# The attention layer of a four-layer graph network: products of two steps grouped, chain stages cut elsewhere, the last 1024 nodes split by block

## The chip, the cores and the metric

The kernel runs on one core of one Trainium2 chip. The metric is the device time of one execution in microseconds (us). The engines are named as in the profile: PE (TensorE; PEld is its weight load), DVE (VectorE), ACT (ScalarE), POOL (GpSimd) and SP (SyncE, which only issues DMAs here). Each engine works through its own queue in order. A name with a q, such as PEq, is an engine's sequencer.

## The reference

Four graph layers on 4096 nodes with 128 features; `adj` is a 4096 x 4096 float32 matrix. After each layer `x = layernorm(x + layer(x))`.

- Layer 0: a signed attention over the graph. Layer 1: two Chebyshev convolutions of order 3 with ELU.
- Layer 2, "the third layer" of this study, is a four-head attention (heads h of 32 features):

```
hp      = (x @ weight.T), seen as (n, 4, 32)
C[n,m]  = alpha_src[m] + alpha_dst[n]          (per head)
tau     = adj.T * exp(max(0.2 C, C))
z       = sum over n of adj.T * (tau / tau_sum) * hp,  + bias
```

- Layer 3: `h @ W_self + (adj @ h / deg) @ W_neigh`, with `deg` the row sums of `adj`.

## The kernel before, in words

Sources are cut into 32 tiles of 128 nodes (`nt`), targets into 8 blocks of 512 (`IB`) or 4 wide blocks of 1024 (`WB`). A matrix `adjT` is read in chunks of 1 MB (512 x 512), `adj` in 1 MB tiles of 2 x 128 sources by 1024 targets. Both land in one ring of five buffers (`ld`, tile `chunk`); SP issues these loads in order, each when its buffer is free.

Layers 0 and 1 run first, up to the product with `w` (L861), the last big product of layer 1. This product is the **block loop** (L855): for each of 8 blocks `ib`, 32 matmuls over 8 chunks into one PSUM bank `pp`. From there on the order of PE, DVE, ACT and POOL is written out by hand: inside `manual_schedule` (L795 to L904) each of these engines gets its instructions in the order in which the program emits them. Four kinds of work are interleaved.

1. **Chains**: generators in a queue, advanced by one stage with `one(chains)`. `block_end` (L588) finishes a block of layer 1: ELU (the helper at L498), transposes, statistics, normalization, `xT`, and with it the per-source factors `es`, `cs` and features `hc` of layer 2. `block_targets` (L629) makes the per-target factors `dv`. `targets` (L669) spreads them over partitions into `D`. `finish` (L712) divides numerators by denominators; `layer3_blocks` (L732) normalizes and multiplies with the weights of layer 3, giving `y`. All of them use one PSUM bank, `px`.
2. **Steps** (L682): one source tile for one pass. A pass (class `Heads`) is 2 heads for 1024 targets; there are 8 passes of 32 steps, 256 in all. A step has two `scalar_tensor_tensor` on DVE (L688, 128 x 1024, `max(D, es) * a`) that give `tau`, and `tau2 = tau * a`, of which DVE makes 704 columns (L691) and POOL 320 (L692) and 1024 (L693). `a` is a PSUM copy of the `adj` tile, made by ACT (L666), which sums the degrees beside it. `tau` and `tau2` have three buffers each. The first two passes go in turn and share a load and a copy for their first 24 source tiles.
3. **Products** (L696, L823): four matmuls of 32 columns each for the denominators (from `tau`) and four for the numerators (from `tau2`), side by side in PE's columns, summed over the pass in the PSUM banks `den` and `num`. After each step PE does the denominators of the step before it and the numerators of the one before that.
4. **Pieces**: single matmuls of the layer-3 product `adj @ y` (L759) for 1024 sources at a time. `credit` (L886) lets 1.3 of them in after each step. They begin when `layer3_blocks` of a wide block has run. What a product sums in PSUM goes into `acc3` (L773, L775). The last 1024 sources' product (L905) comes after the hand-ordered part and also makes the output (`layer3_out`, L780).

In the block loop, 1 step follows a chunk (2 the last) from block 3 on, for source tiles whose block has been finished. PSUM has eight banks: `den`, `num`, `pp`, `px`, two for `a`, two for the first pass's sums, which later become the second `a`.

Of the kernel before, what the change touches and what calls it, by code (L numbers as in the profile page):

```python
# [11 lines left out]
F32 = mybir.dt.float32  # L12
# [7 lines left out]
P = 128  # L20
# [13 lines left out]
def adj_resnorm_d4(ctx: ExitStack, tc: tile.TileContext, x_in, xT_in, adj, adjT, w0g, w0gT, a0, w1a, b1a,  # L34
# [56 lines left out]
    deg = const.tile([P, NT, NW], F32, name="deg")  # L91
# [383 lines left out]
    def network(usual):  # L475

        with ExitStack() as whole:
# [98 lines left out]

            ps_nd = enter(name="ps_nd", bufs=1, space=PSUM)
# [9 lines left out]

            def block_end(ib, p):  # L588
# [3 lines left out]
                oT = l1w.tile([P, IB], F32, name="t2T")  # L592
                nc.vector.tensor_add(oT, p, h0T[:, blk])
# [19 lines left out]
                yield  # L613
                yield
                for half in range(2):
                    two = slice(ib * TB + 2 * half, ib * TB + 2 * half + 2)
                    pn = ps_x.tile([P, 2, F + H], F32, name="px")
                    for k in range(2):
                        t = ib * TB + 2 * half + k
                        nc.tensor.matmul(pn[:, k, :], xT[:, t * P:(t + 1) * P], W2S, start=True, stop=True)  # L620
                    nc.scalar.activation(cs[:, two, :], pn[:, :, F:F + H], AF.Exp, scale=0.2)
                    nc.scalar.activation(es[:, two, :], pn[:, :, F:F + H], AF.Exp, scale=0.8)
                    for k in range(2):
                        t = ib * TB + 2 * half + k
                        nc.vector.tensor_mul(hc[:, t], pn[:, k, 0:F].rearrange("p (h f) -> p h f", f=FO),
                                             cs[:, t, :][:, :, None].to_broadcast([P, H, FO]))
                    yield

            def block_targets(ib):  # L629
# [9 lines left out]
                nc.vector.tensor_sub(d, d, dv[:, blk])  # L639
                nc.scalar.copy(dv[32:64, blk], d[32:64, :])  # L640
                nc.scalar.copy(dv[64:96, blk], d[64:96, :])
                yield
                nc.vector.tensor_sub(d[64:96, :], d[64:96, :], dv[64:96, blk])
                nc.scalar.copy(dv[64:96, blk], d[64:96, :])
                yield
# [4 lines left out]
            class Heads:  # L650
# [3 lines left out]
                def __init__(self, mp, hp):  # L654
                    self.mp, self.hp = mp, hp
                    self.D, self.made = None, 0
                    self.sums = ps_first if (mp, hp) == (0, 0) else ps_nd

                def load(self, nt):

                    if nt % 2 == 0:
                        self.a2 = ld.tile([P, 2, WB], F32, name="chunk")
                        nc.sync.dma_start(self.a2, adj[self.mp, nt // 2])
                    a = self.a2[:, nt % 2, :]
                    ap = ps_a[nt % len(ps_a)].tile([P, WB], F32, name="a")
                    nc.scalar.activation(ap, a, AF.Copy, accum_out=deg[:, nt, self.mp:self.mp + 1])  # L666
                    return a, ap

                def targets(self, mbs=range(2)):  # L669
                    if self.D is None:  # L670
                        self.D = l2w.tile([P, 2, 2, IB], F32, name="D", bufs=2)
                    for mb in mbs:
                        for h in range(2):
                            d = ps_x.tile([P, IB], F32, name="px")
                            nc.tensor.matmul(d, selD[:, 2 * self.hp + h, :],
                                             dv[:, self.mp * WB + mb * IB:self.mp * WB + (mb + 1) * IB],
                                             start=True, stop=True)
                            nc.scalar.copy(self.D[:, h, mb, :], d)
                            self.made += 1
                            yield  # L680

                def step(self, nt, a, ap):  # L682

                    assert self.made == 4
                    tau = l2w.tile([P, 2, WB], F32, name="tau", bufs=3)
                    tau2 = l2w.tile([P, 2, WB], F32, name="tau2", bufs=3)
                    for h in range(2):
                        nc.vector.scalar_tensor_tensor(tau[:, h, :], self.D[:, h].rearrange("p b i -> p (b i)"),  # L688
                                                       es[:, nt, 2 * self.hp + h:2 * self.hp + h + 1], ap,
                                                       op0=ALU.max, op1=ALU.mult)  # L690
                    nc.vector.tensor_tensor(tau2[:, 0, 0:OWN], tau[:, 0, 0:OWN], ap[:, 0:OWN], ALU.mult)  # L691
                    nc.gpsimd.tensor_tensor(tau2[:, 0, OWN:WB], tau[:, 0, OWN:WB], a[:, OWN:WB], ALU.mult)  # L692
                    nc.gpsimd.tensor_tensor(tau2[:, 1, :], tau[:, 1, :], a, ALU.mult)  # L693
                    return tau, tau2

                def product(self, is_den, nt, r):  # L696
# [5 lines left out]
                    for h in range(2):  # L702
                        for mb in range(2):
                            q = 32 * (2 * h + mb)
                            nc.tensor.matmul(acc[q:q + 32, :], weights(nt, 2 * self.hp + h, is_den),  # L705
                                             r[:, h, mb * IB:(mb + 1) * IB], start=nt == 0, stop=nt == NT - 1)
                    if nt == NT - 1:
                        if is_den:
                            self.nd = l2w.tile([P, 2, IB], F32, name="nd")
                        nc.scalar.copy(self.nd[:, int(is_den), :], acc)  # L710

                def finish(self):  # L712
# [5 lines left out]
                    yield  # L718
                    q = transpose4(ps_x, "px", lambda k: self.nd[:, 0, k * P:(k + 1) * P])
                    yield  # L720
                    z = l2w.tile([P, TB, 2, 2, FO], F32, name="z")
                    nc.vector.tensor_mul(z.rearrange("p k h b f -> p (k h b) f"),
                                         q.rearrange("p k (g f) -> p (k g) f", f=FO),
                                         rd.rearrange("p k g -> p (k g)")[:, :, None].to_broadcast([P, TB * 4, FO]))
                    for mb in range(2):
                        xb = x[:, (2 * self.mp + mb) * TB:(2 * self.mp + mb + 1) * TB,
                               2 * self.hp * FO:(2 * self.hp + 2) * FO].rearrange("p k (h f) -> p k h f", f=FO)
                        eng = nc.vector if (self.mp, self.hp) == (NW - 1, H // 2 - 1) else nc.gpsimd
                        eng.tensor_tensor(xb, z[:, :, :, mb, :], xb, ALU.add)
                    yield  # L730

            def layer3_blocks(mp):  # L732
# [3 lines left out]
                for j in range(2):  # L736
                    b = 2 * mp + j
                    q = transpose4(ps_x, "px", lambda k: x[:, b * TB + k, :])
                    xb = l2w.tile([P, TB, P], F32, name="xb", tag="z")
# [5 lines left out]
                    yield  # L745
                    nc.vector.reciprocal(sj, sj)
                    for half in range(2):
                        q = ps_x.tile([P, 2, 2, F], F32, name="px")
                        for k in range(2):
                            nc.tensor.matmul(q[:, k].rearrange("p s f -> p (s f)"), xb[:, 2 * half + k, :],  # L750
                                             W3.rearrange("p s f -> p (s f)"), start=True, stop=True)
                        for k in range(2):
# [4 lines left out]
                        yield  # L757

            def layer3_product(mp):  # L759


                for ib in range(NB):
                    blk = slice(ib * IB, (ib + 1) * IB)
                    last = mp == NW - 1
                    p = (ps_nd.tile([P, IB], F32, name="num") if last and ib % 2 else ps_p.tile([P, IB], F32, name="pp"))
                    for c in range(2):
                        a = chunk(ld, adjT, ib, 2 * mp + c)
                        for k in range(TB):
                            nc.tensor.matmul(p, y[:, (2 * mp + c) * TB + k, :], a[:, k, :],  # L769
                                             start=c == 0 and k == 0, stop=c == 1 and k == TB - 1)  # L770
                            yield c == 1 and k == TB - 1
                    if mp == 0:
# [20 lines left out]

            acc3 = state.tile([P, N], F32, name="acc3", tag="yn")
            with tc.manual_schedule(engines={mybir.EngineType.PE, mybir.EngineType.DVE, mybir.EngineType.Activation,  # L795
# [4 lines left out]
                passes = [Heads(mp, hp) for mp in range(NW) for hp in range(H // 2)]  # L800
                held = NT - 2 * TB
                todo = deque((heads, nt) for nt in range(held) for heads in passes[0:2])
                todo += [(heads, nt) for heads in passes[0:2] for nt in range(held, NT)]
                todo += [(heads, nt) for heads in passes[2:] for nt in range(NT)]
                steps = len(todo)
                ahead = passes[0].load(0)
                credit = 0.0
# [10 lines left out]
                def start_product(mp):  # L818
                    pieces.append(layer3_product(mp))
                    return  # L820
                    yield

                def products():  # L823

                    if len(behind) > 1:
                        heads, nt, tau, _ = behind[-2]
# [116 lines left out]
```

The softmax here doesn't subtract the row's maximum and nothing guards it: scores larger than these inputs give would overflow.

## Time and profile before

| what | before |
|---|---|
| median of 6 runs | 2281.26 us (2277.09 to 2282.76) |
| the profiled execution, whole | 2284.24 us |
| its span, first to last instruction | 2282.3 us |
| busy in the span: PE, PEld | 2175.7, 843.2 us |
| busy: DVE, ACT, POOL | 1176.7, 593.6, 836.9 us |
| mean granted PE clock | 0.99 |
| `w` product (block loop) | from 1113 to 1465 us |
| steps (L688 to L691) | from 1211 to 2189 us |
| end of the span | 2282 us |

A timeline line reads: start, duration, engine, source line, operation, output<-inputs, shapes, count, and in brackets how long the engine stood idle before it and what released it. A line of the chain of waits has start, duration and the engine and line that held the end back in that stretch. A window line has the stretch, its length and the busy time of each engine with the number of instructions. PE's busy time includes instructions that are queued in the array, so a full PE need not be at its peak. A float32 matmul appears as two records.

### The profile page before, as it was taken

The numbers are of one execution on the slowest core, as the hardware profiler recorded it, in microseconds if no ns is written. First come the engines' busy times: TensorE is split into PE (matmuls) and PEld (weight loads), VectorE is DVE, ScalarE is ACT, GpSimd is POOL, SyncE is SP. The second block draws the span as 40 slices with busy tenths as digits, with TensorE's granted clock in tenths as the row PEclk, the third lists the DMA queues.
The fourth block names the chain that finished last, engine by engine and source line by source line (L and its number), as shares of the span: only waits on it lengthen the run. The fifth ranks groups of instructions, "written<-read, shape, count | busy, mean of one in ns | idle before, by whom it ended". The sixth has DMA issues, their size and how long they took to land.

```text
span 2282.3 us, 22715 instructions
## 1 busy us (share of the span) xinstructions
PE 2175.7 (95%) x8552; PEld 843.2 (37%) x8552; DVE 1176.7 (52%) x1709; ACT 593.6 (26%) x1012; POOL 836.9 (37%) x540
## 2 busy tenths in 40 slices
PE   3899999999999999999999999969999999999998
PEld 2333444444444444444443333312222322232233
DVE  4544463000001100000025776779999999999955
ACT  4755200000000000000032222334444443443320
POOL 0000000000000000000004565669999999999930
PEclk9799999999999999999999999999999999999999
DMA  7886647888776677777776555434666666666665
GB/s 266 331 330 237 221 170 267 300 298 303 265 270 229 235 264 238 267 263 275 273 243 226 216 185 210 177 111 148 221 247 241 232 238 244 243 234 241 236 225 204
DMA packets 83608, 549.14 MB, mean 241 GB/s; under 512 B 9376, under 2 KB 15520, under 8 KB 17568
## 3 DMA queue, kind: packets, MB, share of 16 engines
q1 hardware_dynamic: 75200, 542.15, 67.4%
q10 hardware_dynamic: 8288, 5.44, 0.8%
q8 instruction: 69, 1.13, 0.2%
q14 instruction: 51, 0.42, 0.1%
HBM read 545.46 MB, written 2.10 MB: 240 GB/s over the span
## 4 chain that ended last, share of the span: by engine, by line
PE 83%; DVE 10%; issue 3%; ACT 2%; DMA 2%; ACTq 0%; POOL 0%; DVEq 0%; POOLq 0%
PE pacc L514 29%; PE pacc L346 10%; PE den L705 9%; PE pp L769 9%; PE pp L861 8%; PE num L705 7%; DVE tau L688 5%; DVE tau L691 2%; PE pmm L540 2%; PE num L769 1%; PE pden L334 1%; PE num L861 1%; PE px L135 1%; PE ptr L135 1%; ACT a L666 1%
## 5 line engine op out<-in xcount | busy, mean ns | idle before, releaser
L688 DVE SCALAR_TENSOR_TENSOR tau<-D,es,a 128x1024 f32<-128x1024 f32 x512 | 629.2, 1268 | 27.7 <-ACT a L666 27.5
L693 POOL TENSOR_TENSOR tau<-tau,chunk 128x1024 f32<-128x1024 f32 x256 | 609.1, 2379 | 16.6 <-DVE tau L688 15.8
L612 POOL TENSOR_TENSOR x<-x,B2R 128x512 f32<-128x512 f32 x8 | 10.2, 1280 | 1180.8 <-PE px L135 1180.8
L705 PE MATMUL den<-tau,cs 128*32 128x512 f32 x2048 | 357.4, 608 | 30.8 <-DVE tau L688 22.9
L666 ACT ACTIVATE a<-chunk 128x1024 f32<-128x1024 f32 x232 | 238.7, 1029 | 453.2 <-DVE tau L691 387.8
L705 PE MATMUL num<-tau,hc 128*32 128x512 f32 x2048 | 346.4, 599 | 0.6 <-POOL tau L693 0.6
L692 POOL TENSOR_TENSOR tau<-tau,chunk 128x320 f32<-128x320 f32 x256 | 222.5, 869 | 155.7 <-DVE tau L688 106.3
L769 PE MATMUL pp<-chunk,xT 128*128 128x512 f32 x448 | 236.1, 629 | 0.0
L691 DVE TENSOR_TENSOR tau<-tau,a 128x704 f32<-128x704 f32 x256 | 223.9, 875 | 0.0
L514 PE MATMUL pacc<-chunk,t 128*128 128x512 f32 x512 | 223.5, 592 | 0.0
L514 PE MATMUL pacc<-chunk,v 128*128 128x512 f32 x512 | 222.5, 592 | 0.0
L514 PE MATMUL pacc<-chunk,x 128*128 128x512 f32 x512 | 221.9, 593 | 0.0
L861 PE MATMUL pp<-chunk,w 128*128 128x512 f32 x448 | 208.1, 602 | 2.4 <-ACT xT L565 1.6
L346 PE MATMUL pacc<-chunk,hw 128*128 128x512 f32 x408 | 196.3, 621 | 2.3 <-DVE hw L411 2.3
L705 PEld LDWEIGHTS den<-tau,cs 128*32 128x32 f32 x2048 | 58.1, 107 | 270.0 <-DVE tau L688 179.7
L705 PEld LDWEIGHTS num<-tau,hc 128*32 128x32 f32 x2048 | 88.9, 110 | 145.0 <-issue 131.5
L514 PEld LDWEIGHTS pacc<-chunk,v 128*128 128x128 f32 x512 | 97.2, 190 | 122.0 <-issue 122.0
L514 PEld LDWEIGHTS pacc<-chunk,x 128*128 128x128 f32 x512 | 96.4, 190 | 116.7 <-issue 116.7
L514 PEld LDWEIGHTS pacc<-chunk,t 128*128 128x128 f32 x512 | 96.1, 190 | 115.3 <-issue 115.3
L769 PEld LDWEIGHTS pp<-chunk,xT 128*128 128x128 f32 x448 | 71.7, 188 | 158.6 <-issue 144.3
L561 DVE COPY w<-ptr 128x512 f32<-128x512 f32 x8 | 5.5, 691 | 241.5 <-PE ptr L135 241.5
L861 PEld LDWEIGHTS pp<-chunk,w 128*128 128x128 f32 x448 | 80.5, 190 | 115.5 <-issue 111.4
(190 smaller groups left out, 1442.7 us busy)
## 6 DMA issues: line engine op xcount, KB each, us to landing
chunk<-in_adjT SPq DMA_DIRECT2D x386, 1024.0 KB, 4.8
chunk<-in_adj SPq DMA_DIRECT2D x116, 1024.0 KB, 4.8
keep<-in_adjT SPq DMA_DIRECT2D x13, 1024.0 KB, 6.9
xT<-in_xT ACTq DMA_DIRECT2D x8, 256.0 KB, 6.3
out<-o ACTq DMA_DIRECT2D x8, 256.0 KB, 4.3
W1A<-in_w1a ACTq DMA_DIRECT2D x1, 384.0 KB, 5.9
W1B<-in_w1b ACTq DMA_DIRECT2D x1, 384.0 KB, 6.7
W0T<-in_w0gT ACTq DMA_DIRECT2D x1, 64.0 KB, 5.6
```

The lines of the kernel that those rows point to most:

```text
L135: nc.tensor.transpose(p[:, k, :], src(k), ident)
L346: nc.tensor.matmul(p, hw[:, j * TB + k, :], a[:, k, :], start=first and k == 0, stop=last and k == TB - 1)
L514: nc.tensor.matmul(p, stationary(c * TB + k), a[:, k, :], start=n == 0 and k == 0, stop=n == NB - 1 and k == TB - 1)
L540: nc.tensor.matmul(ph, W1A[:, k, hh * P:(hh + 1) * P], r, start=k == 0, stop=k == 2)
L666: nc.scalar.activation(ap, a, AF.Copy, accum_out=deg[:, nt, self.mp:self.mp + 1])
L688: nc.vector.scalar_tensor_tensor(tau[:, h, :], self.D[:, h].rearrange("p b i -> p (b i)"), es[:, nt, 2 * self.hp + h:2 * self.hp + h + 1], ap,
L691: nc.vector.tensor_tensor(tau2[:, 0, 0:OWN], tau[:, 0, 0:OWN], ap[:, 0:OWN], ALU.mult)
L692: nc.gpsimd.tensor_tensor(tau2[:, 0, OWN:WB], tau[:, 0, OWN:WB], a[:, OWN:WB], ALU.mult)
L693: nc.gpsimd.tensor_tensor(tau2[:, 1, :], tau[:, 1, :], a, ALU.mult)
L705: nc.tensor.matmul(acc[q:q + 32, :], weights(nt, 2 * self.hp + h, is_den), r[:, h, mb * IB:(mb + 1) * IB], start=nt == 0, stop=nt == NT - 1)
L769: nc.tensor.matmul(p, y[:, (2 * mp + c) * TB + k, :], a[:, k, :], start=c == 0 and k == 0, stop=c == 1 and k == TB - 1)
L861: nc.tensor.matmul(p, w[:, c * TB + k, :], a[:, k, :], start=c == 0 and k == 0, stop=c == NB - 1 and k == TB - 1)
```

## The change

Five edits, all in layer 2 and what follows it; line numbers above are those of the kernel before.

- **Products**: two steps are emitted, then one group: the numerators of the older pair's second step, denominators and numerators of the new pair's first step, denominators of its second step. Pieces follow by credit, 2.67 for a pair, and 4 for a pair in the last pass; after the end of a product's sum (`wait`) the accumulation goes in after the next step.
- **Chain stages** now end just after PE's instructions, and what the other engines do with them opens the next stage. `block_end`'s first stage (the ELU, now with `min`, `Exp`, `Relu` in that order) is emitted at once, ahead of the group. `block_targets` works in place in PSUM.
- **Block loop**: steps stand ahead of the chunk's matmuls and halfway through them. Blocks 4 to 7 have five cuts with two steps each (10 steps), block 3 four (8). A step's load and copy are emitted right before it.
- **First two passes** go in turn to the end and share all loads and copies.
- **Last 1024 nodes**: two passes of 4 heads for 512 targets each (`Pass` with `wide` false) replace two of 2 heads for 1024. A step there has four `scalar_tensor_tensor` of 512 columns; the `tau2` parts keep their sizes as 2 x 352, 2 x 160 and 2 x 512; two steps share one `a` tile; loads are two DMAs of half the columns. Block 6's layer-3 product then becomes pieces within block 7's pass, and only block 7's remains for the end.

```diff
             def block_end(ib, p):
                 oT = l1w.tile([P, IB], F32, name="t2T")
+                r = l1w.tile([P, IB], F32, name="elu_r")
+                n = l1w.tile([P, IB], F32, name="elu_n")
                 nc.vector.tensor_add(oT, p, h0T[:, blk])
-                elu(oT, oT, B1B)
+                nc.vector.tensor_scalar(n, oT, B1B, 0.0, op0=ALU.add, op1=ALU.min)
+                nc.scalar.activation(n, n, AF.Exp)
+                nc.scalar.activation(r, oT, AF.Relu, bias=B1B)
+                nc.vector.scalar_tensor_tensor(oT, n, -1.0, r, op0=ALU.add, op1=ALU.add)
                 yield
                 q = transpose4(ps_x, "px", lambda k: oT[:, k * P:(k + 1) * P])
+                yield
                 nc.vector.tensor_add(x[:, tb, :], q, x[:, tb, :])
...
+                q = transpose4(ps_x, "px", lambda k: x[:, ib * TB + k, :])
                 yield
-                q = transpose4(ps_x, "px", lambda k: x[:, ib * TB + k, :])
                 nc.scalar.copy(xT[:, blk], q.rearrange("p k i -> p (k i)"))
...
                         nc.tensor.matmul(pn[:, k, :], xT[:, t * P:(t + 1) * P], W2S, start=True, stop=True)
+                    yield
                     nc.scalar.activation(cs[:, two, :], pn[:, :, F:F + H], AF.Exp, scale=0.2)
...
             def block_targets(ib):
-                d = l1w.tile([96, IB], F32, name="elu_r")
-                nc.scalar.activation(d, pd, AF.Exp, scale=-0.8)
-                nc.scalar.copy(dv[:, blk], d)
                 yield
+                nc.scalar.activation(pd, pd, AF.Exp, scale=-0.8)
+                nc.scalar.copy(dv[:, blk], pd)
                 yield
-                nc.vector.tensor_sub(d, d, dv[:, blk])
+                nc.vector.tensor_sub(pd, pd, dv[:, blk])
...
+                    for q in range(0, 4, n):
+                        head = self.parts[q][0]
+                        nc.vector.scalar_tensor_tensor(flat(tau[:, q:q + n]), flat(self.D[:, q:q + n]),
+                                                       es[:, nt, head:head + 1], ap, op0=ALU.max, op1=ALU.mult)
...
+                        own = OWN // 2
+                        rep = lambda v, q: v[:, None, :].to_broadcast([P, q, v.shape[1]])
+                        nc.vector.tensor_tensor(tau2[:, 0:2, 0:own], tau[:, 0:2, 0:own], rep(ap[:, 0:own], 2), ALU.mult)
+                        nc.gpsimd.tensor_tensor(tau2[:, 0:2, own:IB], tau[:, 0:2, own:IB], rep(a[:, own:IB], 2), ALU.mult)
+                        nc.gpsimd.tensor_tensor(tau2[:, 2:4, :], tau[:, 2:4, :], rep(a, 2), ALU.mult)
...
-                passes = [Heads(mp, hp) for mp in range(NW) for hp in range(H // 2)]
-                held = NT - 2 * TB
+                passes = [Pass([2 * mp, 2 * mp + 1], [2 * hp, 2 * hp + 1]) for mp in range(NW - 1) for hp in range(H // 2)]
+                passes += [Pass([b], list(range(H))) for b in range(NB - 2, NB)]
...
+                def products():
+                    if len(behind) > 2:
+                        this, nt, _, tau2 = behind.popleft()
+                        num(this, nt, tau2)
+                    this, nt, tau, tau2 = behind.popleft()
+                    this.product(True, nt, tau)
+                    num(this, nt, tau2)
+                    this, nt, tau, _ = behind[0]
+                    this.product(True, nt, tau)
...
+                    cuts = [0, 2, 4, 6, 8] if ib < 4 else [0, 2, 4, 5, 6, 8]
+                    for first, last in zip(cuts, cuts[1:]):
+                        ks = [(c, k) for c in range(first, last) for k in range(TB)]
+                        for n, (c, k) in enumerate(ks):
+                            if ib > 2 and n in (0, len(ks) // 2):
+                                if n == 0:
+                                    load()
+                                step()
...
+                            if n + 1 in (len(ks) // 2, len(ks)) or ib <= 2 and k % 2:
                                 one(chains)
+                        if last == NB:
+                            end = block_end(ib, p)
+                            next(end)
+                            chains.append(end)
...
+                        if ib > 2:
+                            products()
+                load()
...
                 while todo:
                     step()
-                    credit = min(credit + 1.3, 2.0) if pieces else 0.0
-                    while credit >= 1.0:
+                    if wait:
+                        wait = bool(pieces) and not one(pieces)
...
+                    load()
                     one(chains)
+                    step()
+                    load()
+                    products()
+                    one(chains)
+                    credit = min(credit + (4.0 if todo and todo[0][0] is passes[-1] else 2.67), 4.0) if pieces else 0.0
+                    while credit >= 1.0 and pieces and not wait:
                         credit -= 1.0
-                        if one(pieces):
-                            credit = 0.0
-                    one(chains)
...
-            for _ in layer3_product(NW - 1):
+            for _ in layer3_product(this.blocks):
                 pass
```

More of the change, by code (lines that the diff above doesn't have):

```diff
@@ L682, in step @@
                 def step(self, nt, a, ap):
                     assert self.made == 4
[L685 to L690, printed above, removed]
@@ L840, in step @@
                 def step():
-                    nonlocal ahead
-                    heads, nt = todo.popleft()
-                    tau, tau2 = heads.step(nt, *ahead)
+                    this, nt = todo.popleft()
+                    assert nt // TB in ended
+                    tau, tau2 = this.step(nt, *ahead)
+                    behind.append((this, nt, tau, tau2))
                     if nt == NT - 1:
-                        later = passes.index(heads) + 2
+                        later = passes.index(this) + 2
@@ L846, in step, with num @@
                         if later < len(passes):
                             chains.append(passes[later].targets())
-                    if todo and not (todo[0][1] == nt and heads is passes[0]):
-                        ahead = todo[0][0].load(todo[0][1])
-                    behind.append((heads, nt, tau, tau2))
-                    products()
-                ready = 0
+                def num(this, nt, tau2):
+                    this.product(False, nt, tau2)
+                    if nt == NT - 1 and this is not passes[-1]:
+                        if this is passes[0]:
+                            first_sums.close()
+                            ps_a.append(enter(name="ps_a2", bufs=1, space=PSUM))
+                        chains.append(this.finish())
+                        if this.heads[-1] == H - 1:
+                            chains.append(layer3_blocks(this.blocks))
+                            chains.append(start_product(this.blocks))
@@ L899, in network @@
                 nc.vector.reciprocal(rdeg, rdeg)
-                for chain in (heads.finish(), layer3_blocks(NW - 1)):
+                for chain in (this.finish(), layer3_blocks(this.blocks)):
                     for _ in chain:
```

207 lines of the change are left out of this document (97 added, 110 removed).

## The prediction, made before the changed kernel had been run

> **What bounds the kernel now.** I read the busy windows of the attention part first, then the timeline of a few steps in it, then the chain of waits at its two ends. Before 1113 us (layers one and two up to `w`) nothing changes.
>
> The windows give stretch, length, busy time and count of PE, PEld, DVE, ACT, POOL, then granted clock, DMA share, GB/s:
>
> ```profile
> 1400.00:1450.00 50.00, 47.71 (x223) 16.54 (x221) 33.93 (x45) 14.34 (x27) 27.73 (x18) 1.00 0.56 196
> 1450.00:1500.00 50.00, 38.87 (x194) 11.97 (x190) 35.74 (x47) 13.81 (x26) 30.98 (x20) 0.93 0.35 126
> 1600.00:1700.00 100.00, 98.99 (x570) 28.98 (x568) 100.00 (x98) 42.43 (x79) 99.63 (x65) 1.00 0.63 228
> 1900.00:2000.00 100.00, 99.34 (x571) 28.30 (x570) 100.00 (x99) 38.96 (x68) 98.36 (x63) 1.00 0.68 247
> ```
>
> In the 1400s PE leads, around 1500 nobody does, and from 1600 PE, DVE and POOL all look full. The timeline tells these three apart:
>
> ```profile
> 1703.61 2.46 DVE L688 SCALAR_TENSOR_TENSOR tau<-D,es,a 128x1024 f32<-128x1024 f32 x2
> 1705.99 0.88 DVE L691 TENSOR_TENSOR tau<-tau,a 128x704 f32<-128x704 f32 x1
> 1706.79 2.46 DVE L688 SCALAR_TENSOR_TENSOR tau<-D,es,a 128x1024 f32<-128x1024 f32 x2
> ```
>
> DVE starts a step every 3.18 us without a gap (two instructions 1.19 apart, then 0.80); POOL's two take 3.16. On PE the chain of waits gives 1.00 for the four denominator matmuls, 0.86 for the four numerators and 1.06 for one piece of the layer-3 product, 2.91 together, and 0.86 more when there are two pieces. A full matmul is two records of 0.43, that is 0.86; four narrow ones side by side also take 0.86. The excess is changeover: 0.14 into the narrow ones, 0.20 back. At 1.3 pieces a step PE needs 3.17. So **DVE bounds** from 1538 (59th step) to 2189 (256th): 198 x 3.18 = 629 of 651 us, the other 22 being DVE's own chain work. PE has almost the same load but does not hold DVE up.
>
> Before that PE bounds, with a hole at every block's end:
>
> ```profile
> 1303.82 3.65 PE pp L861 x8
> 1307.49 0.70 DVE t2T L593
> 1308.21 0.72 ACT elu_r L501
> 1308.94 0.53 ACT elu_n L503
> 1309.49 0.69 DVE t2T L504
> 1310.18 2.40 DVE tau L688 x2
> ```
>
> The next step's DVE work is queued behind the block's ELU, which waits for PE's last matmul. PE has one held step to do and then starves: some 3.3 us a block. Blocks 4 to 7 take 209.0 us (1255.7 to 1464.7), 52.25 each, with 9 steps each. The drain after them is slow because each of the last 16 steps of the first two passes loads and copies its own `a` into one PSUM buffer:
>
> ```profile
> 1495.57 0.88 DVE L691 TENSOR_TENSOR tau<-tau,a 128x704 f32<-128x704 f32 x1
> 1496.49 1.03 ACT L666 ACTIVATE a<-chunk 128x1024 f32<-128x1024 f32 x1 [3.40 <-DVE tau L691]
> 1497.74 2.47 DVE L688 SCALAR_TENSOR_TENSOR tau<-D,es,a 128x1024 f32<-128x1024 f32 x2 [1.28 <-ACT a L666]
> ```
>
> 4.56 a step (1493.18 to 1497.74), 1.38 of it DVE waiting for the copy. From 2189.0, the last step's end, to 2282.3 is the tail: 93.3 us, bound by PE at 7.45 a block (16 records, 6.87, and transposes, 0.58).
>
> **The change, part by part.** The times are the profiled execution's (span 2282.3, 2284.24 whole); the median of the six runs is 2281.26, 3 less, and I take the difference over to it.
>
> *Block loop.* `load` leaves the place before the loop, where its ACT copy (1.15) stood ahead of `xT` on the chain: -1.2. Block 3 goes from 47.4 us to 27.5 + 8 x 1.72 + 4 x 0.34 + 2.6 = 45.2 on PE, taken 46: -1.4. Blocks 4 to 7 have 10 steps in 5 groups: PE 27.5 + 17.2 + 1.7 + 2.6 (transposes, `px`, `pd`) = 49.0, the floor. DVE: 10 x 3.18, 5 x 1.38 for the copy, 6.5 of chain work (add 0.60, ELU 1.1, x add 0.69, statistics 1.6, `hc` 1.0, rest 1.5) = 45.2, to which come waits for ACT: the ELU's 1.2, the square root's 0.4 and the normalization's 1.65, which now stands ahead of the next `a` copy in ACT's queue: 48.5. The ELU is now queued behind two steps, where POOL is at work. A row that shows what this can cost:
>
> ```profile
> 1509.40 2.37 POOL L693 TENSOR_TENSOR tau<-tau,chunk 128x1024 f32<-128x1024 f32 x1 [0.27 <-DVE tau L688]
> 1510.03 2.28 DVE L639 TENSOR_TENSOR elu_r<-elu_r,dv 96x512 f32<-96x512 f32 x1
> ```
>
> With POOL idle that line takes 0.69 (its minimum); here it ends half a microsecond after POOL's. Three of a block's instructions read SBUF this way (clamp, ELU sum, mean), so 0 to 1.6 each, which puts the ceiling at 53.3; L639 itself moves to PSUM and is in the 6.5 at 0.60. The second `px` matmul now follows `hc` of the first within one stage: nothing if DVE is ahead, else `es`, `cs` and `hc`, 0.9. So floor 49, ceiling 54. SP's queue gets each step's load ahead of its chunks; at a DMA share of 0.56 and 4.8 to land I cost that at nothing, five buffers covering it (a late one would show as ACT's copy waiting for a DMA, 4.8 at most). The Trainium skill speaks of the port in "SBUF — State Buffer", Who interferes with whom: the loser of the shared port waits for the whole other instruction. By that rule each could wait up to POOL's 2.4, an estimate of 56 a block. From the rows, and nearer to the floor since POOL is not always in its long instruction, I take 51: -5 (-13 to +7), and 48 steps are done at the loop's end near 1457, where before there were 44. The hole at the block's end goes, since `products` follows the ELU with 3.4 us of held matmuls; if DVE is late there, the hole returns.
>
> *Drain.* Before, from 1464.7 to the 64th step's end at 1555.8: 91.1 us for 20 steps. After, 16 steps in 8 pairs sharing `a`: 2 x 3.18 + 1.38 = 7.74, with 5 more for the last ELU, 67 in all: -24 (-18 if all chain work adds up, -28 if it fits the copy waits).
>
> *Products of two steps together, in the 128 wide steps.* PE per pair: 4 x 0.86 + 0.34 + 2.67 x 0.86 = 6.07 against DVE's 6.36. It was no bound before, so this is 0; what hides it is DVE's load. If DVE were 0.3 a pair faster, PE would be late next.
>
> *Last 1024 nodes as two passes of four heads.* 64 steps have four 512-element instructions in place of two of 1024. That form is not in the trace. Nearest: L785, same operation, 332 ns at 128, and 1265 at 1024: 1.04 ns an element and 199 fixed, of which about 75 overlap, so 0.66 each; the low end is L775's 0.60 for 512, the high end 0.73, nothing overlapping. 4 x 0.66 + 0.80 = 3.43, so +0.25 x 64 = **+16** (+1 to +35; the elements stay the same, so there is no gain, and I take the fit, which is drawn through the same operation). The skill's "VectorE: DVE Perf Modes", The TRN2 errata — SBUF-src ops pay a fixed extra latency per instruction, speaks against this part too: small tiles pay the fixed cost anew, about 150 cycles; by that, an estimate of +20. POOL's pieces keep their sizes (320 and 1024), and L612 with a repeated operand is on its line (1280 for 512), so POOL stays under 3.43. ACT's copies halve and 20 MB of loads go (with the drain's), both off the path. The narrow load is two DMAs in 2 KB runs, a form not in the trace; at twice the 4.8 us it would still land within the 13.7 of the four steps that it serves, so 0; if it were three times as long, some 0.2 a step. Counting the loop out, the product of blocks 4 and 5 gives 28 pieces in the first narrow pass, and 36 plus 26 of block 6's 32 fall in the second, at four a pair: PE 3.58 + 0.20 + 3.43 = 7.2 against 6.9, about 118 us either way with chains. DVE's added chain work: statistics of one block 1.7 and 8 more accumulations of 0.60: **+6.5**.
>
> *Tail.* Only block 7 is left: up to its `y` 13.7 (2189.0 to 2202.7), first product 3.4, last add to end 10.6, and 7 periods between. PE alone would do 4.01 (3.43 + 0.58); DVE in its present order needs 1.51 from add to first output and 3.95 to the next add, 5.45. I take 5.2: 36.4. With 1 for leftovers, 65 against 93.3: **-28** (-37 to -22).
>
> Sum: -1.2 - 1.4 - 5 - 24 + 0 + 16 + 6.5 - 28 = -37. So 2284.2 becomes 2247, and the median 2281.3 becomes **2244**.
>
> **Rivals.** *The block loop turns DVE-bound*, with the port waits above: blocks at 54 (+12): 2256. For: DVE sums to 48.5 without them, PE to 49.0. Against: held matmuls cover some. *Everything goes well*: narrow instructions at 0.60 (-15), tail at 4.0 (-8): 2221. *The last passes give nothing*: block 6's product is not hidden (its accumulations wait in DVE's queue), the tail stays, and the rest brings -9: 2272. *Slower*: the ring of three. A pair's last denominator holds its `tau`, and the next pair's POOL work needs the third `tau2`, freed by the numerator that opens the next group. That group may start from 3.0 to about 6.9 us after its pair (first tau2 product at 4.9, POOL free at 8.0 and needing one numerator by then). If the pieces make it later, DVE and POOL stand in every pair of the steady part. It decides at 42 us over 104 pairs, 6.76 instead of 6.36; at 7.2, PE's time with four pieces, it costs 87: 2331. Against: PE's 6.07 leaves 0.3 a pair to catch up.
>
> **How the numbers follow.** Forecast 0.50, DVE-bound loop 0.18, all well 0.13, nothing from the last passes 0.09, slower 0.10. The range 2220 to 2272 takes in all but the last and the edges; the unknown costs' far ends (narrow instructions at +35, blocks at 49) lie within it one at a time. A measurement here tells 0.2%, 4.6 us, from no change. Faster: 0.50 + 0.18 + 0.13 + 0.06 = 0.87; same 0.03; slower 0.10.
>
> **What would show it.** Right: DVE at 6.36 a pair from about 1530 on, loop end near 1457, no PE gap after a block's last matmul, 512-wide steps near 3.43, tail near 65 with DVE fuller than PE. Wrong: DVE waiting for PE or POOL in the steady part, ELU instructions over 2 us, block periods above 53, or pieces of block 6 after the last step.

## The result, and the profile after

The changed kernel takes 2289.27 us (median of 20 runs, 2281.21 to 2292.22), the kernel before 2280.34 in the runs beside it (45 runs): a ratio of 1.0038, 95% interval [1.0029, 1.0047]. It is slower by 0.4% where the forecast was 1.6% faster. Its profiled execution has a span of 2285.2 us.

From the timelines of both kernels I took the end of the DVE instruction that closes the 64th, 192nd, 224th and 256th step (before L691, after L712 and L718) and made stages of them:

| stage, us | before | after | difference | forecast |
|---|---|---|---|---|
| start to the 64th step | 1555.9 | 1520.0 | -35.9 | -31.6 |
| 128 wide steps (65 to 192) | 420.1 | 447.0 | +26.9 | 0 |
| steps 193 to 256 (after: 512 wide) | 213.0 | 260.5 | +47.5 | +22.5 |
| tail, to the span's end | 93.3 | 57.7 | -35.6 | -28 |
| sum | 2282.3 | 2285.2 | +2.9 | -37.1 |

So both ends gained more than forecast, and the steady middle lost 74 (26.9 and 47.5), where 22.5 were forecast. First the windows of the changed kernel in the stretches that were shown of the kernel before (columns as there):

```profile
1400.00:1450.00 50.00, 49.13 (x243) 18.51 (x242) 38.77 (x51) 15.23 (x29) 33.27 (x22) 1.00 0.60 211
1450.00:1500.00 50.00, 38.81 (x225) 9.58 (x223) 41.02 (x53) 16.47 (x31) 35.86 (x23) 0.90 0.27 100
1600.00:1700.00 100.00, 95.75 (x534) 27.88 (x533) 89.71 (x87) 37.61 (x68) 90.28 (x59) 1.00 0.69 246
1900.00:2000.00 100.00, 89.48 (x520) 25.62 (x516) 96.53 (x109) 31.03 (x62) 92.93 (x60) 0.97 0.57 199
```

In the 1400s TensorE went from 47.71 to 49.13 of 50 us: the holes at the ends of the blocks are gone. In the 1600s, where DVE had been busy for 100.00 of 100, it is busy for 89.71. The bound engine now stands still for 10%, and no other engine has become fuller instead: PE went from 98.99 to 95.75, POOL from 99.63 to 90.28. The timeline at a block's end shows the gain:

```profile
1296.65 4.46 PE L896 MATMUL pp<-chunk,w 128*128 128x512 f32 x10
...
1301.03 1.07 PE L730 MATMUL num<-tau,hc 128*32 128x512 f32 x8
1301.14 0.69 DVE L598 TENSOR_TENSOR t2T<-pp,xT 128x512 f32<-128x512 f32 x1 [0.81 <-PE pp L896]
...
1303.66 0.69 DVE L602 SCALAR_TENSOR_TENSOR t2T<-elu_n,elu_r 128x512 f32<-128x512 f32 x1 [1.31 <-ACT elu_r L601]
```

While the ELU runs, TensorE works off held products (L730, from 1301.03 on). Five such additions (L598) lie between 1251.1 and 1451.2, four blocks apart: 50.0 us a block, before 52.25.

The timeline of the wide steps shows the first loss:

```profile
1641.83 2.74 PE L792 MATMUL pp<-chunk,xT 128*128 128x512 f32 x6
...
1643.14 0.88 DVE L712 TENSOR_TENSOR tau<-tau,a 128x704 f32<-128x704 f32 x1
...
1644.60 0.59 ACT L795 COPY acc<-pp 128x512 f32<-128x512 f32 x1 [4.42 <-PE pp L792]
1645.09 1.03 ACT L685 ACTIVATE a<-chunk 128x1024 f32<-128x1024 f32 x1
...
1646.32 2.47 DVE L708 SCALAR_TENSOR_TENSOR tau<-D,es,a 128x1024 f32<-128x1024 f32 x2 [2.31 <-POOL tau L714]
```

Read it from the bottom. DVE starts a step 2.31 us late. The label names POOL, but what DVE needs and gets last is the copy of the chunk, `a`, which ACT does only from 1645.09 to 1646.12. ACT had nothing else to do, but this copy stood in its queue behind L795, which takes a finished sum of the layer-3 product out of PSUM (its evacuation; the expectations below call it the evacuation of a finished piece). And L795 had waited 4.42 us for the last of the sum's pieces on TensorE. The table of waits counts these:

```profile
ACT acc L795 <- PE pp L792: 38.9, 8, 6.0
DVE tau L708 <- POOL tau L714: 15.8, 8, 2.6
```

Eight waits of ACT (38.9 us) became eight of DVE (15.8 us). The code says why: `wait` makes the loop evacuate a finished sum between the first step of a pair and the `load()` of the second, and ACT takes its instructions in order. For the first product over sources this evacuation is a copy on ACT (L795), for the later ones an addition on DVE (L797).

The second loss is in the 512-wide passes:

```profile
2053.19 2.72 DVE L708 SCALAR_TENSOR_TENSOR tau<-D,es,a 128x512 f32<-128x512 f32 x4 [0.85 <-issue]
...
2056.62 2.71 DVE L708 SCALAR_TENSOR_TENSOR tau<-D,es,a 128x512 f32<-128x512 f32 x4
2059.26 0.88 DVE L718 TENSOR_TENSOR tau<-tau,a 128x704 f32<-128x704 f32 x1
...
2060.17 0.60 ACT L685 ACTIVATE a<-chunk 128x512 f32<-128x512 f32 x1 [6.46 <-DVE tau L718]
...
2060.80 0.58 ACT L685 ACTIVATE a<-chunk 128x512 f32<-128x512 f32 x1
2060.98 2.72 DVE L708 SCALAR_TENSOR_TENSOR tau<-D,es,a 128x512 f32<-128x512 f32 x4 [0.84 <-issue]
```

A step without a wait takes what was forecast: 3.43 us from 2053.19 to 2056.62. But the copies for two steps go into the two halves of one PSUM tile (`ap2`). The step at 2056.62 is the first of such a pair, the one at 2060.98 the second. The second one's copy (2060.17) goes into the free half, and yet it waits until DVE's last read of the first half (L718, up to 2060.14) is done; DVE then stands still for 0.84 until the copy is there. The copy right behind it (2060.80) is for the next pair and goes into the other tile. So two steps take 7.79 (2053.19 to 2060.98) where 6.86 was to be had.

In the very last pass there is a third loop, 8.09 us long. The chain of waits shows TensorE's part of it:

```profile
2193.70 1.75 PE den L730 x8
2195.44 3.63 PE pp L792 x8
2199.07 1.00 PE num L730 x8
```

The four pieces (eight records) end at 2199.07, and DVE's accumulation L797 starts at 2199.11 (the one before it at 2191.02). Behind it on DVE stands the second step of the pair; the denominator waits for that step's `tau`, the next four pieces for the denominator, and the next accumulation for the pieces. By the timeline, from accumulation to accumulation: 0.61 until the step begins, 2.63 until its `tau` is made, 1.18 until the denominator is done and 3.63 for the pieces, 8.05 together.

### The profile page after: what moved, and what is told of

It reads as the page before. It is cut to its first block, busy times and chain, and to the rows that moved or that the text cites. A ratio compares the mean times of both kernels' runs of the same rounds, so it can differ in the third digit from the quotient of the medians.

```text
span 2285.2 us, 22868 instructions
## 1 busy us (share of the span) xinstructions
PE 2146.5 (94%) x8552; PEld 848.2 (37%) x8552; DVE 1189.0 (52%) x1844; ACT 550.0 (24%) x996; POOL 839.5 (37%) x539
## 5 line engine op out<-in xcount | busy, mean ns | idle before, releaser
L708 DVE SCALAR_TENSOR_TENSOR tau<-D,es,a 128x1024 f32<-128x1024 f32 (+1 forms) x640 | 646.6, 1059 | 73.7 <-ACT a L685 29.7
L730 PE MATMUL den<-tau,cs 128*32 128x512 f32 x2048 | 342.2, 607 | 6.2 <-DVE tau L708 4.6
L730 PE MATMUL num<-tau,hc 128*32 128x512 f32 x2048 | 318.9, 619 | 13.1 <-POOL tau L714 11.4
L685 ACT ACTIVATE a<-chunk 128x1024 f32<-128x1024 f32 (+1 forms) x224 | 202.2, 903 | 459.5 <-DVE tau L712 235.6
L792 PE MATMUL pp<-chunk,xT 128*128 128x512 f32 x480 | 226.8, 607 | 1.3 <-DVE acc L797 1.3
L713 POOL TENSOR_TENSOR tau<-tau,chunk 128x320 f32<-128x320 f32 x192 | 167.4, 872 | 143.6 <-DVE tau L708 90.0
L712 DVE TENSOR_TENSOR tau<-tau,a 128x704 f32<-128x704 f32 x192 | 168.5, 878 | 0.0
L730 PEld LDWEIGHTS den<-tau,cs 128*32 128x32 f32 x2048 | 81.3, 112 | 197.7 <-issue 103.8
L730 PEld LDWEIGHTS num<-tau,hc 128*32 128x32 f32 x2048 | 59.6, 110 | 224.3 <-issue 105.0
L792 PEld LDWEIGHTS pp<-chunk,xT 128*128 128x128 f32 x480 | 85.0, 189 | 131.4 <-issue 128.1
```

What stands on the lines that cost most here:

```text
L685: nc.scalar.activation(ap, a, AF.Copy, accum_out=deg[:, nt, s:s + 1])
L708: nc.vector.scalar_tensor_tensor(flat(tau[:, q:q + n]), flat(self.D[:, q:q + n]), es[:, nt, head:head + 1], ap, op0=ALU.max, op1=ALU.mult)
L712: nc.vector.tensor_tensor(t2[:, 0:OWN], t[:, 0:OWN], ap[:, 0:OWN], ALU.mult)
L713: nc.gpsimd.tensor_tensor(t2[:, OWN:WB], t[:, OWN:WB], a[:, OWN:WB], ALU.mult)
L730: nc.tensor.matmul(acc[32 * q:32 * q + 32, :], weights(nt, head, is_den), r[:, q, :], start=nt == 0, stop=nt == NT - 1)
L792: nc.tensor.matmul(p, y[:, c * TB + k, :], a[:, k, :], start=c == blocks[0] and k == 0, stop=end)
```

## The experiments

Each run below gives its median and, with a 95% interval, its ratio to the kernel before in the runs beside it. There were three such groups (e1 to e4, e5 to e7, e8 and e9), with medians of the kernel before of 2280.39, 2278.72 and 2282.90 us, so whole times of different groups compare to some 4 us; where less is at stake, the stages of the profiles are compared.

**Theory A**: the loss is three waits made by the order of the queues and by a shared tile: ACT's copy of the sums ahead of the next `a` copy, one PSUM tile for two steps, and the accumulation between the two steps. **Theory R**, the prediction's slower rival: products of two steps together hold the ring of three `tau`/`tau2` buffers. **Theory N**: 512-wide passes cost more than their short tail returns.

**Own tile for each step of the last passes** (e1).

```
-  if nt % 2 == 0:
-      self.ap2 = ps_a[nt // 2 % 2].tile([P, WB], F32, name="a").rearrange(...)
-  ap = self.ap2[:, nt % 2, :]
+  ap = ps_a[nt % 2].tile([P, WB], F32, name="a")[:, 0:IB]
```

> Every step of the last two passes gets a PSUM tile of its own for its chunk, where two steps shared one. Theory A (the change made three waits: ScalarE's copies of the sums stand ahead of the next chunk copy in the 128 wide steps, two steps share one chunk tile in the last two passes, the accumulation between two steps closes a loop in the very last pass): only the second goes. The pair of steps in the first 512-wide pass falls from 7.8 to about 6.95 us and its 0.84 us idle on DVE is gone; the last pass, which the third wait holds, stays near 8.1. 16 pairs x 0.84 = 13 us: about 2276, ratio to the kernel before near 0.998. Theory R (tau and tau2 buffers, held two steps longer by the joined products, stall DVE): the idle time stays, about 2289.

2275.24 us, 0.9981 [0.9968, 0.9993]. The first 512-wide pass went from 128.7 to 116.6 us, and the idle times of 0.84 are gone; the last pass went only from 131.8 to 129.6, and its last pairs still take 8.09. As theory A had it.

**Load ahead of the evacuation** (e2). The second step's copy of the chunk now comes before L795 in ACT's queue.

```
-  if wait:
-      wait = bool(pieces) and not one(pieces)
...
   load()
   one(chains)
+  if wait:
+      wait = bool(pieces) and not one(pieces)
   step()
```

> The load and copy of the next step's chunk are put ahead of the evacuation of a finished piece of the last layer, where the evacuation stood first. Theory A: the eight idle times of 1.8 to 2.6 us on DVE in the 128 wide steps go (15.8 us), since ScalarE no longer waits for the last piece with the next chunk copy behind it; about 2273, ratio near 0.997. Theory R: the idle times stay, since the buffers cause them; about 2289. The last two passes are as they were in either.

2271.00 us, 0.9962 [0.9947, 0.9977]. The wide steps take 431.7 us, 15.3 less. The same place in its timeline:

```profile
1639.50 1.03 ACT L685 ACTIVATE a<-chunk 128x1024 f32<-128x1024 f32 x1 [0.69 <-DVE tau L712]
...
1642.52 2.51 DVE L708 SCALAR_TENSOR_TENSOR tau<-D,es,a 128x1024 f32<-128x1024 f32 x2
...
1643.23 0.58 ACT L795 COPY acc<-pp 128x512 f32<-128x512 f32 x1 [2.58 <-PE pp L792]
...
1645.70 2.51 DVE L708 SCALAR_TENSOR_TENSOR tau<-D,es,a 128x1024 f32<-128x1024 f32 x2
```

ACT still waits for the last piece (19.1 us in all), but DVE no longer waits for ACT there: its copy was done at 1640.53, and it goes on at 3.18 a step.

**Last 1024 nodes again as passes of 2 heads x 1024** (e3).

```
-  passes = [... for mp in range(NW - 1) ...]
-  passes += [Pass([b], list(range(H))) for b in range(NB - 2, NB)]
+  passes = [... for mp in range(NW) ...]
-  credit = min(credit + (4.0 if todo and todo[0][0] is passes[-1] else 2.67), 4.0) ...
+  credit = min(credit + 2.67, 4.0) ...
```

> The last edit alone undone: the last 1024 nodes again as two passes of 2 heads x 1024 nodes, the rest as changed. By the traces: 64 steps at about 3.2 to 3.35 us instead of 260.5 us in all, so -46 to -56, and a tail like the one of the kernel before (93.3 us where the changed kernel has 57.7), +36. Theory A: about 2270 to 2279, with the eight idle times still there; so the narrow passes as they stand cost 10 to 20 us more than they save. Theory N (512-wide passes are only as dear as their instructions, and their tail pays for it): 2295 or more.

2267.42 us, 0.9953 [0.9938, 0.9968]: steps 193 to 256 take 215.5 us (-45.0), the tail 84.8 (+27.2; the expectation had +36 from the 93.3 of the kernel before; that the moved chain stages made the difference is likely, not shown). So the narrow passes as they stood cost 18 us by these stages and 22 by the medians. What the expectation calls theory N, that they pay as they stand, is out. Theory N as worded above agrees with this run as well as theory A does.

**Evacuation behind the second step and its load** (e4).

```
-  if wait:
-      wait = bool(pieces) and not one(pieces)
...
   step()
   load()
+  if wait:
+      wait = bool(pieces) and not one(pieces)
   products()
```

> The evacuation of a finished piece of the last layer is put behind the second step of the pair and its load, ahead of the products. Theory A: the eight idle times of the wide steps go (-16) as with the load alone put ahead, and the last pass is no longer closed in a loop through the accumulation: its pair falls from 8.1 to between 7.4 and 7.8 (still held by the shared chunk tile), -5 to -11. About 2263 to 2268. Theory R: about 2289, the idle times stay. If only the position of ScalarE's copy matters and the loop in the last pass is TensorE's own load, it equals the kernel with the load put ahead, about 2273.

2269.83 us, 0.9963 [0.9951, 0.9975]: the wide steps went to 428.8, as expected, but the last pass did not get faster (133.1 us; a pair with an accumulation takes 8.40). The number was a miss. The timeline shows idle times of 0.84 in nearly every pair there, so the shared tile took the third wait's place: two steps, 0.84 and the accumulation. Whether the third wait is real needed both mends.

**Both mends** (e5: e1 and e4 together).

> Both mends: the evacuation of a finished piece behind the second step of the pair and its load, and a PSUM chunk tile for every step of the last two passes. With the evacuation late alone, the pair of the last pass stayed at 8.2 us with 0.84 idle on DVE, which is the shared tile. Theory A, the three waits: with both, the pair there is two steps of 3.43 and one accumulation of 0.7, 7.5, where TensorE needs 4 x 0.86 + 3.63 = 7.1; the pair of the first 512-wide pass is near 6.95. 32 pairs x 0.84 = 27 us less than with the evacuation late alone: about 2243 to 2248, ratio to the kernel before near 0.985. If the last pass is held by TensorE instead (its four pieces and eight products, with their weight changes), the pair stays near 8.0 and the time is about 2257.

**2240.11 us, 0.9833 [0.9810, 0.9856]**: 1.7% faster than the kernel before, about 2% faster than the changed one, and a little better than the 2243 to 2248 expected. The first narrow pass takes 115.9 us, the last 119.2:

```profile
2155.18 0.68 DVE L795 TENSOR_TENSOR acc<-pp,acc 128x512 f32<-128x512 f32 x1
...
2155.78 2.71 DVE L706 SCALAR_TENSOR_TENSOR tau<-D,es,a 128x512 f32<-128x512 f32 x4
2158.41 0.88 DVE L716 TENSOR_TENSOR tau<-tau,a 128x704 f32<-128x704 f32 x1
...
2163.24 2.71 DVE L706 SCALAR_TENSOR_TENSOR tau<-D,es,a 128x512 f32<-128x512 f32 x4
```

2163.24 - 2155.78 = 7.46 a pair, with no idle time of DVE: two steps of 3.43 and one accumulation.

**Own tile and load ahead** (e8: e1 and e2 together): the accumulation stays between the steps.

> A PSUM chunk tile for every step of the last two passes, and the load ahead of the evacuation, which stays between the two steps of a pair (only the kernels with the evacuation late have it behind the second). Theory A: the eight idle times and the 0.84 of the first 512-wide pass go, but the loop of the last pass stays (accumulation, second step, four denominators, four pieces, accumulation): its pair stays at 7.9 to 8.1 and not 7.46. 2289 - 18 - 14 = 2257, some 10 above the sum of 2247 that the pair of 7.46 would give. If where the accumulation stands does not matter, it equals the kernel with both mends, 2240.

2256.49 us, 0.9891 [0.9871, 0.9910], as theory A had it. The last pass takes 129.7 us; the kernel with both mends needs 119.2. DVE stands still for 0.54 to 1.74 us ahead of each accumulation, and at the end the loop is 8.09 long again:

```profile
2182.79 0.69 DVE L795 TENSOR_TENSOR acc<-pp,acc 128x512 f32<-128x512 f32 x1 [0.54 <-PE pp L790]
...
2190.88 0.69 DVE L795 TENSOR_TENSOR acc<-pp,acc 128x512 f32<-128x512 f32 x1 [0.54 <-PE pp L790]
```

With this the third wait stands by itself: 10.5 us.

**Products after every step** (e6) in the loop behind the block loop, the rest as changed (the function `single` itself is left out here):

```
   one(chains)
+  single()      # denominator of the step before, numerator of the one before that
   step()
   load()
-  products()
+  single()
```

> In the loop behind the block loop, the products are issued after every step as in the kernel before, and not for two steps together; all the rest is the changed kernel, the evacuation's place too. Theory A: the eight idle times of the wide steps and the 0.84 of the narrow pairs do not come from the grouping, so no gain: about 2289, or somewhat slower where TensorE is near its bound, from the changeovers that it saves (0.34 us a pair more: up to 5 us in the last two passes). Theory R (grouping holds the three tau and tau2 buffers): the idle times go, about 2266.

2290.79 us, 1.0065 [1.0043, 1.0087]. No gain in sum, but not the same waits either. In the wide steps DVE stands still for 20.1 us, in the changed kernel for 23.6. Its two largest waits there, from 1518.6 to 1962.1 us:

```profile
DVE tau L712 <- PE num L730: 9.8, 10, 2.2
DVE tau L708 <- ACT a L685: 7.4, 5, 2.1
```

The waits for the copy have halved, and waits for a numerator have come in their place. So this run alone doesn't settle theory R. What does are e2 and both mends, which leave the grouping and the ring of three as they are: the idle times go. And in the wide steps no step of DVE waits for a denominator or a numerator, neither there nor in the changed kernel. Theory R is wrong.

**The same on the kernel with both mends** (e9).

> The kernel with both mends, but products after every step as in the kernel before, in the loop behind the block loop. With the waits gone TensorE is what DVE's steps run up against: two changeovers more a pair (0.34 us). In the last pass TensorE then needs 7.1 + 0.34 = 7.45 a pair beside DVE's 7.46, in the wide passes 6.41 beside 6.36, so grouping is worth 0 to 10 us: 2240 to 2250 here. Theory R would have it faster than 2240, since three tau and tau2 are held shorter.

2266.67 us, 0.9932 [0.9910, 0.9953]: 23 to 27 us slower than with both mends, where 0 to 10 were expected. By stages: 4.7 up to the 64th step, 11.8 in the wide steps, 2.8 and 2.7 in the narrow passes, 1.8 in the tail. Much of it comes right behind the two first passes (a line of its timeline, one of its windows and one of its waits):

```profile
1526.56 0.89 DVE L710 TENSOR_TENSOR tau<-tau,a 128x704 f32<-128x704 f32 x1 [4.29 <-PE num L728]
```

```profile
1522.00:1527.00 5.00, 4.67 (x25) 1.10 (x28) 0.71 (x2) 0.86 (x2) 0.40 (x1) 0.56 0.00 0
```

```profile
DVE tau L710 <- PE num L728: 15.8, 12, 4.3
```

DVE waits to write a `tau2` until a numerator has read it, 15.8 us in 12 places; the kernel with both mends has no such wait. So the ring of three does bite in this loop, but when products are issued singly, not together. In the first of these places TensorE ran at a granted clock of 0.56.

This is not the price of single products as such. The kernel before issues them singly too, with its pieces spread over all steps and its chain stages cut elsewhere, and in its wide steps (420.1 us) DVE hardly stands still at all: 0.6 us. What e9 shows is that in the changed loop, where pieces come in bunches behind a pair and a chain's instructions on TensorE can wait ahead of the products, the grouping is needed. In its wide steps TensorE stands still for 49.0 us, with both mends for 23.6; which part of that is the bunches and which the chains was not tried.

**Wide last passes, evacuation late** (e7: e3 and e4 together).

> The last 1024 nodes as two passes of 2 heads x 1024 nodes, with the evacuation behind the second step of the pair: what the narrow passes are worth once the waits are mended is the difference between this and the kernel with both mends. Theory A: the eight idle times go from the 2267 of the wide form, so about 2250, and the narrow passes, mended, are worth 3 to 7 us: 46 to 50 us more tail here against 64 x 0.25 for instructions, 6 to 10 for the chains and 0.35 a step for accumulations there. Theory N: at or below the kernel with both mends.

2245.00 us, 0.9863 [0.9838, 0.9888]. Against both mends: steps 193 to 256 take 214.0 against 235.1 us, the tail 84.4 against 58.3. Mended, the narrow passes save 26.1 and cost 21.1. By the stages theory N is wrong, by 5 us; the whole times, also 5 apart, don't decide it alone, since the two intervals overlap. The expectation had 3 to 7, but by luck: it put the saved tail at 46 to 50 us and the cost at 44 to 48, both 20 or more too high.

## Why the prediction was wrong

**Up to the 64th step: right.** Forecast -31.6, measured -35.9. The other runs with products in pairs, whose code is the same there, put the step between 1516.5 and 1522.9 (their first steps already lie 6 us apart), so 4 us are within what executions differ. A block takes 50.0 (forecast 51), and the block loop ends at 1451, not 1457; from there to the 64th step it takes 68.8 (forecast 67). The feared waits behind POOL did not come: the clamp took 0.49, the ELU's sum 0.69, the means 0.16. POOL had 0.1 us left of its last instruction when the clamp began, and nothing to do till the next step. So the changed kernel does not test the rule of the Trainium skill that was weighed there ("SBUF — State Buffer", Who interferes with whom).

Between the forecast of -37.1 and the +2.9 of the stages lie 40.0 us. Two terms failed, by 26.9 and by 25.0; the other two were better than forecast, by 4.3 and 7.6.

**"Products of two steps together, in the 128 wide steps ... so this is 0": the first step that failed.** It set TensorE's 6.07 a pair against DVE's 6.36, and nothing else. As a comparison of the two engines' work it holds: with the waits mended DVE stands still for 5.1 of 427.2 us there, and never for TensorE's products. But the same edit moved the evacuation of a finished sum between a step and the next load, and ACT, whose work fills 40% of this stage, was taken for a bystander. An engine with little work can hold up others by waiting: 15.3 of the 26.9 us are this (e2), 4.5 more go when the evacuation is behind the second step (e2 against both mends). The 7.1 that remain are 2.6 of added work of DVE and 4.5 of idle time, 3.1 of that in the first two steps after the 64th.

**The last 1024 nodes: the second step that failed. The size of the instructions was right, the waits were put at nothing.** Four instructions of 512 take 2.71, so 0.66 to 0.68 each, and the step 3.43 as forecast, 0.25 more than before or 16 for 64 steps; the estimate of +20 from the Trainium skill's fixed cost ("VectorE: DVE Perf Modes", The TRN2 errata — SBUF-src ops pay a fixed extra latency per instruction) was somewhat high against +16 from the rows. With the chain work 22.5 were forecast for these steps; the kernel with both mends has 22.1. The changed kernel has 47.5. The 25 more are the shared `a` tile, 12.1 in the first pass and 2.2 in the last (e1), and the loop through the accumulation, 10.5 in the last pass (e8 against both mends). For that pass the forecast had TensorE's 7.2 a pair and "about 118 us either way"; 8.1 and 131.8 were measured, and 119.2 with both mends. The diff showed both: the line that makes `ap2` once for two steps, and `wait`'s place ahead of the second step. The prediction counted ACT's copies and called them "off the path", and did not ask who must have finished reading a tile before the next copy.

**Tail: the way right, the size too small.** 57.7 against 65; the last outputs follow each other in 3.87 us, not in the 5.2 that I took for DVE's order. 3.87 is TensorE's four pieces (3.43) and the transposes (0.44): TensorE sets the pace, and the sign "DVE fuller than PE" did not come (26.80 and 26.93 of the 30 us from 2245). Pieces of block 6 did fall behind the last step, which the list of signs had as wrong; they ran in between the chain of block 7, from 2228 to about 2242.

**The rivals.** None of them was it. The slower one named buffers; what came were three other waits, of 0.5 to 2.6 us each. Without them the sum would have been close: the profiled execution of the kernel with both mends takes 2245.2 us, the sum was 2247. In part that is luck: its wide steps take 7 us more than forecast, its tail 7 us less.

## What to carry to other kernels

When a step is moved, write down for each engine the order of its instructions around the new place, and ask of every one that can wait what stands behind it; here an engine with 60% idle time held up the full one. Count a buffer's reuse by who must have read it last, not by its size: half a tile that is free is not free if the tile is the unit that is waited for. And mend waits together before judging a part: taking one of the two away showed next to nothing in the last pass (131.8 us as changed, 133.1 and 129.6 with one mend), both gave 119.2.

## What the runs showed of the hardware

In these traces the granted TensorE clock fell after TensorE had stood still for some microseconds, and the products that came next took longer. In the kernel with both mends it stands still for 3.71 us before 1519.52, waiting for a copy by ACT. In the window from 1519 to 1524 the clock is 0.50, and eight matmul records of a numerator take 1.94 us at 1522.55, against 1.03 at 1525.44. In the window from 1530 to 1540 the clock is 1.00. With single products (e9) TensorE stands still for 6.52, 5.18 and 2.90 us before 1519.81, 1533.71 and 1549.41. In the windows from 1522 to 1527, 1534 to 1537 and 1550 to 1554 the clock is then 0.56, 0.57 and 0.57, each time with DVE waiting for a numerator (4.29, 1.63 and 1.83 us). Here is the second of these places:

```profile
1533.71 0.58 PE L692 MATMUL px<-dv,selD 96*128 96x512 bf16 x1 [5.18 <-ACT D L694]
1534.22 1.94 PE L728 MATMUL den<-tau,cs 128*32 128x512 f32 x8
1535.93 1.38 PE L728 MATMUL num<-tau,hc 128*32 128x512 f32 x8
1537.13 1.03 PE L728 MATMUL den<-tau,cs 128*32 128x512 f32 x8
```

How much of DVE's waits there is the clock, and how much TensorE's standing still before it, was not tried.
